# Projecting x by W1 and W2 during the first load of a four-layer graph kernel, and summing near rows straight into the residual

## The chip, the cores and the metric

The kernel runs on one core of one Trainium2 chip. The metric is the device time of one execution in microseconds (us); several executions are timed and their median is given. The profile is of one execution, whose span (first to last instruction) is a little shorter than its time.

## The reference, cut to what matters

There are N = 2708 nodes with D = 128 features each, and a dense f32 adjacency matrix `adj` of 2708 x 2708 (29 MB). Four graph layers follow one another, each wrapped as `x = layernorm(x + layer(x, adj))`. The change touches the first layer and the wrapping around it:

```python
def _lap_mul(A, x):
    d = 1.0 / jnp.sqrt(jnp.sum(A, axis=-1))
    return d[:, None] * (A @ (d[:, None] * x))

z = leaky_relu(_lap_mul(A, x) @ W1 + b1, negative_slope=0.1)
sq = jnp.sum(z * z, axis=-1)
d2 = jnp.maximum(sq[:, None] + sq[None, :] - 2.0 * (z @ z.T), 0.0)
S = jnp.exp(-jnp.sqrt(d2 + 1e-10) / 2.0)
S = jnp.where(ranks < 4, S, 0.0)      # the 4 nearest of each row
A2 = S + A
out = _lap_mul(A2, x) @ W2 + b2
x = layernorm(x + out)
```

So adj is multiplied twice: first for z, from which the 4 nearest rows of each row are found, and then, with those 4 entries added to each row, for the output. Layer 1 (an attention layer) ranks the rows by a score `c` that is computed from the x of layer 0; layers 2 and 3 each multiply adj once more.

## The kernel before, in words

Rows are cut into T = 22 tiles of 128 (the last, tile FULL = 21, has LAST = 20 rows). The columns of a product over all nodes are cut into C = 6 chunks: four of 512, one of 384 and one of 276 columns; `chunk_tiles` tells which row tiles a chunk covers (4, 4, 4, 4, 3 and 3). Products with adj have the transposed form: a tile of 128 rows of features is the stationary operand, 128 x 512 of adj (transposed in memory) streams past it, and a chunk's sum over all tiles stands in one PSUM bank `acc` (six of them; two further banks `mis` serve all else in the first stages). All matmuls are f32, and each is recorded in two parts. Six of the 22 row tiles of adj (`res`) stay in SBUF; the 16 others are streamed for each pass in panels of 4 tiles x 512 columns (`load_panel`, L157).

*The load and the first pass* (L425 to L504). For each chunk of columns, x (`load_x`) and the panels arrive by DMA. VectorE adds the panels up (`both`, L443 to L448), a matmul with `ones` (L460) turns that into row sums, the degrees; `inv_sqrt` makes `dinv`, and `scale_rows` writes `y = dinv * x` (L469). TensorE, in an order written out by hand (`manual_schedule`), forms what products it has data for (L392): a panel of chunk c can be used for the tiles whose `dinv` is known. When all is loaded, the panels that are still missing are fetched again (`rest`). At the end of a chunk, `finish` copies the sum to `hT`, `make_z` multiplies it by W1 (L344) and forms z and its norm on VectorE, `turn_z` transposes z back (L362), and `split_norms`/`turn_norms` cut the norm into three bf16 parts and turn them to a row (L371 to L384). Such later steps are queued in `Due`: `due.at(n, f)` runs f when the n-th product has been issued, `tick` counts products.

*The neighbour search* (L555 to L582). For each row tile, six bf16 matmuls with the norms (L564) and six f32 matmuls of z (L574) fill the six banks; ScalarE copies them to `key` (three buffers), and VectorE finds the eight largest and their places (L576, L577). `weigh` (L520), called for three groups of tiles, turns them to similarities `sim`, adds them to the degree, and writes `y2 = d2inv * x` to SBUF and to memory (`y2_rows`). The first groups are multiplied on GpSimd, the last on VectorE.

*Pass 2* (`by_panels`, L171, called at L776). The products of y2 with adj (L186), chunk by chunk. Beside them GpSimd fetches, for each row tile, the 4 nearest rows by 4 indirect DMAs (`sum_near`, L597; 16 buffers `got`), VectorE sums them weighted by `sim` into `near_sum` (L608, L610), and TensorE adds that to the chunk's sum by a matmul with the identity (`add_near`, L614). Then, per chunk: copy to `hT` (L733), `norm0` (times W2, add to x and b2, layer norm; L644), `turn` (transpose, L660), `find_c` (the score c, L668), and per tile `compare` (which scores are greater, L687), `rank_rows`, `rank_columns` and `times_w`. The numbers in `near_at` (L723) and in `end_pass2` say at which product each of these is issued. TensorE, VectorE and ScalarE work strictly in that order in this stage. Once all ranks are known, layer 1 goes on.

Of the kernel before, what the change touches and what calls it, by code (L numbers as in the profile page):

```python
# [50 lines left out]
def kernel(  # L51
# [73 lines left out]

    def load_x(ts):
        t0, t1 = ts[0], min(ts[-1] + 1, FULL)
        nc.sync.dma_start(xs[:, t0:t1, :], x[t0 * P : t1 * P, :].rearrange("(t p) d -> p t d", p=P))
        if t1 <= ts[-1]:
            nc.sync.dma_start(xs[:LAST, FULL, :], x[FULL * P :, :])  # L130
# [15 lines left out]
    hT = big.tile([P, N], F32, tag="hT", name="hT")  # L146
# [24 lines left out]
    def by_panels(weights, done, tick=None, ready=(), first=None, behind=None):  # L171
# [8 lines left out]
        def product(c, i, src, w):  # L180
# [4 lines left out]
            stop = tick is None and i == (FULL if c % GROUPS == 0 else FULL - 1)  # L185
# [51 lines left out]
    def add_bias(b):  # L237
        nc.vector.tensor_add(xs, xs, b[:, None, :].to_broadcast([P, T, D]))
# [26 lines left out]
    y = big.tile([P, T, D], F32, tag="y", name="y")  # L265
# [63 lines left out]
    with tc.tile_pool(name="knn", bufs=1) as knn:  # L329
        nsq = knn.tile([P, T], F32, tag="nsq", name="nsq")  # L330
        nsq3 = knn.tile([3, N], BF16, tag="nsq3", name="nsq3")
# [3 lines left out]
        nc.vector.memset(nsq, 0.0)  # L335
# [3 lines left out]
        zs = {}  # L339

        def make_z(ts):
            po = mis_tile()
            for k, t in enumerate(ts):
                nc.tensor.matmul(  # L344
                    po[: pw[t], k * D : (k + 1) * D], lhsT=hT[:, t * P : t * P + pw[t]], rhs=w1_sb, start=True, stop=True
                )
            for k, t in enumerate(ts):
                p = pw[t]
                z = zs[t] = knn.tile([P, D], F32, tag="z", name="z", bufs=8)
                nc.vector.scalar_tensor_tensor(  # L350
                    z[:p], po[:p, k * D : (k + 1) * D], dinv[:p, t : t + 1], b1_sb[:p], op0=ALU.mult, op1=ALU.add
                )
                nc.vector.scalar_tensor_tensor(z[:p], z[:p], 0.1, z[:p], op0=ALU.mult, op1=ALU.max)
                junk = small.tile([P, D], F32, tag="junk", name="junk")
                nc.vector.scalar_tensor_tensor(
                    junk[:p], z[:p], -1.0, z[:p], op0=ALU.mult, op1=ALU.mult, accum_out=nsq[:p, t : t + 1]
                )

        def turn_z(c, ts):
            pt = mis_tile()  # L360
            for k, t in enumerate(ts):
                nc.tensor.transpose(pt[:, k * P : k * P + pw[t]], zs[t][: pw[t]], ident[: pw[t], : pw[t]])  # L362
            nc.scalar.copy(zT[:, cols[c]], pt[:, : cw[c]])

        def split_norms(c, ts):

            t0, w = ts[0], len(ts)
            parts = small.tile([P, 4, 3], F32, tag="parts", name="parts")
            rest = small.tile([P, 4], F32, tag="rest", name="rest")
            part_b = small.tile([P, 4], BF16, tag="part_b", name="part_b")  # L370
            nc.vector.tensor_copy(rest[:, :w], nsq[:, t0 : t0 + w])  # L371
            for n in range(3):
                nc.vector.tensor_copy(part_b[:, :w], rest[:, :w])
                nc.vector.tensor_copy(parts[:, :w, n], part_b[:, :w])
                if n < 2:
                    nc.vector.tensor_sub(rest[:, :w], rest[:, :w], parts[:, :w, n])
            return parts

        def turn_norms(c, ts, parts):
            ps = mis_tile()  # L380
            for t in ts:
                o = t * P - starts[c]
                nc.tensor.transpose(ps[:3, o : o + pw[t]], parts[: pw[t], t - ts[0], :], ident[: pw[t], : pw[t]])
            nc.scalar.copy(nsq3[:, cols[c]], ps[:3, : cw[c]])  # L384
# [6 lines left out]
        def add(c, i, src, first=False, last=False):  # L391
            nc.tensor.matmul(accs[c][:, : cw[c]], lhsT=y[:, i, :], rhs=src[:, : cw[c]], start=first, stop=last)  # L392
# [12 lines left out]
        def add_few():  # L405
            for c in range(C):
                nc.tensor.matmul(
                    accs[c][:, : cw[c]], lhsT=y[few(c), FULL, :], rhs=res[few(c), FULL - S, cols[c]],
# [4 lines left out]
        def finish(c):  # L413
            ts = chunk_tiles[c]
            nc.scalar.copy(hT[:, cols[c]], accs[c][:, : cw[c]])
            due.at(due.n + 2, make_z, ts)
            due.at(due.n + 8, turn_z, c, ts)

            def norms():
                parts = split_norms(c, ts)  # L420
                due.at(due.n + 4, turn_norms, c, ts, parts)

            due.at(due.n + 7, norms)

        G = S // 4  # L425
        with (
            tc.tile_pool(name="load", bufs=4) as load,
            tc.tile_pool(name="degp", bufs=2) as degp,
            tc.manual_schedule(engines={nc.tensor.engine}),
        ):  # L430
            wait = None
            for c in range(C):
# [15 lines left out]
                nc.vector.tensor_add(both[:, 0, :w], both[:, 0, :w], both[:, 1, :w])  # L448

# [7 lines left out]
                ts = chunk_tiles[c]  # L457
# [11 lines left out]
                scale_rows(y, xs, dinv, ts)  # L469
                if c == C - 1:  # L470
                    spread(y[:, FULL, :])
                wait = (c, c, parts[c] if c < G else None, c == C - 1)
                if c == C - 2:
                    w1_sb = load_const(w1, D, "w1")
                    w2_sb = load_const(w2, D, "w2")
# [4 lines left out]
                    b1_sb = load_rows(b1, D, "b1")  # L480
# [24 lines left out]


# [10 lines left out]

        y2 = big.tile([P, T, D], F32, tag="y", name="y2")

        def weigh(ts):  # L520
# [14 lines left out]
            if t1 < T:  # L535
                nc.gpsimd.tensor_mul(  # L536
                    y2[:, t0:t1, :], xs[:, t0:t1, :], d2inv[:, t0:t1, None].to_broadcast([P, t1 - t0, D])
# [626 lines left out]
```

## Time and profile before

| what | us |
|---|---|
| time, median of 3 executions | 1121.94 (1120.0 to 1123.04) |
| span of the profiled execution | 1119.4 |
| TensorE busy (matmul) | 1044.2 |
| VectorE busy | 642.7 |
| ScalarE busy | 306.1 |
| GpSimd busy | 299.4 |

By stage (busy us of each engine in the stretch, and the share of the DMA engines):

| stretch (us from the span's start) | TensorE | VectorE | ScalarE | GpSimd | DMA |
|---|---|---|---|---|---|
| 0 to 56, load | 25.85 | 41.70 | 1.69 | 12.45 | 0.99 |
| 56 to 98.8, load | 42.60 | 33.32 | 0.62 | 0 | 0.97 |
| 98.8 to 149.8, rest of the first pass | 51.00 | 20.48 | 9.21 | 0 | 0.42 |
| 149.8 to 294, neighbour search | 142.69 | 136.36 | 79.04 | 5.63 | 0.03 |
| 294 to 301.8, into pass 2 | 6.39 | 3.84 | 1.42 | 3.80 | 0.65 |
| 301.8 to 414, pass 2 | 109.18 | 64.47 | 31.33 | 87.22 | 0.70 |
| 414 to 438, end of pass 2 | 13.58 | 19.70 | 12.36 | 3.60 | 0.11 |
| 438 to 1119, all later stages | 652.94 | 322.83 | 170.44 | 186.71 | |

The granted clock of TensorE is its share of full speed[...]. In a timeline each line is a run of like instructions: start, duration, engine, source line, operation, output and inputs, shapes, count, and in brackets the idle time before it with what ended it.

### The profile page before, as it was taken

Reading aid. Unit: us, or ns where it says so; the run is one execution under the profiler, and the core shown is the slowest. Engines: PE = TensorE matmul, PEld = TensorE weight load, DVE = VectorE, ACT = ScalarE, POOL = GpSimd, SP = SyncE. Lnnn points to the kernel's source line nnn. Section 1 sums busy time; section 2 is a strip of 40 time slices with the busy share of each in tenths; the row PEclk is TensorE's granted clock in tenths of the full one; section 3 lists DMA queues with packets and bytes.
Section 4 is the critical chain, followed back from the end, with each engine's and each line's share of the span. In section 5 each row is a group of like instructions: output and inputs, shape, how many; then the busy total and the mean of one; then the engine's idle time right before and its main releaser. Section 6 shows DMA issues by size and latency. Waiting matters only on the chain.

```text
span 1119.4 us, 10743 instructions
## 1 busy us (share of the span) xinstructions
PE 1044.2 (93%) x3495; PEld 494.5 (44%) x3495; DVE 642.7 (57%) x1381; ACT 306.1 (27%) x569; POOL 299.4 (27%) x296
## 2 busy tenths in 40 slices
PE   0899999999999975999799999998999999999997
PEld 0346544444345654333333333333444644465445
DVE  6885549999636679403099999997311212122132
ACT  0000145555202434000165656664110100011000
POOL 4000000000477772772355655660010100000000
PEclk9999999999999995999999999998999999998999
DMA  9996320000576660797545534454475766563754
GB/s 349 354 316 222 125 101 1 1 0 1 178 274 201 184 207 13 230 304 236 164 121 148 176 96 129 164 171 142 150 236 186 227 227 219 173 227 117 263 166 129
DMA packets 110245, 193.89 MB, mean 173 GB/s; under 512 B 14156, under 2 KB 47106, under 8 KB 109926
## 3 DMA queue, kind: packets, MB, share of 16 engines
q1 hardware_dynamic: 91046, 151.12, 40.7%
q0 software_dynamic: 19136, 42.01, 12.0%
q8 instruction: 29, 0.48, 0.2%
q14 instruction: 34, 0.28, 0.1%
HBM read 217.20 MB, written 4.30 MB: 198 GB/s over the span
## 4 chain that ended last, share of the span: by engine, by line
PE 51%; issue 4%; DMA 4%; DVE 2%; POOL 1%; ACT 1%; POOLq 0%; DVEq 0%; ACTq 0%
PE acc L186 32%; PE hacc L977 8%; PE num L1048 8%; DMA rows<-in_adjT,slot_i 2%; DMA part<-in_adjT 1%; PE mis L259 1%; POOL rows L1035 1%; DVE mask L692 1%; PE mis L1110 0%; PE mis L1063 0%; DMA got<-y_rows,where 0%; ACT junk L710 0%; ACT hT L220 0%; PE mis L1076 0%; DVE mask L697 0%
## 5 line engine op out<-in xcount | busy, mean ns | idle before, releaser
L186 PE MATMUL acc<-part,y 128*128 128x512 f32 (+2 forms) x384 | 156.0, 550 | 2.1 <-DMA part<-in_adjT 1.6
L1035 POOL DMA_INDIRECT rows<-in_adjT,slot_i x86 | 120.7, 1404 | 107.9 <-PE num L1048 79.9
L1048 PE MATMUL num<-rows,lw 128*64 128x512 f32 (+2 forms) x516 | 117.0, 558 | 6.7 <-DMA rows<-carry 3.7
L977 PE MATMUL hacc<-err,xws 128*128 128x512 f32 (+3 forms) x264 | 113.6, 567 | 2.2 <-DVE err L972 1.8
L574 PE MATMUL acc<-zT,z 128*128 128x512 f32 (+4 forms) x264 | 106.9, 552 | 0.0
L602 POOL DMA_INDIRECT got<-y_rows,where x88 | 93.0, 1057 | 29.6 <-issue 11.9
L186 PEld LDWEIGHTS acc<-part,y 128*128 128x128 f32 x384 | 70.4, 191 | 64.5 <-issue 53.9
L970 DVE TENSOR_TENSOR err<-inv,num 128x1024 f32<-128x1024 f32 (+1 forms) x88 | 74.5, 856 | 27.1 <-DMA rows<-in_adjT,slot_i 21.0
L966 ACT ACTIVATE inv<-num 128x1024 f32<-128x1024 f32 (+1 forms) x88 | 64.3, 734 | 88.4 <-PE num L1048 86.6
L575 ACT COPY key<-acc 128x512 f32<-128x512 f32 (+3 forms) x132 | 70.2, 534 | 58.1 <-issue 29.8
L392 PE MATMUL acc<-part,y 128*128 128x512 f32 (+2 forms) x192 | 82.4, 582 | 2.2 <-DVE y L233 2.2
L977 PEld LDWEIGHTS hacc<-err,xws 128*128 128x128 f32 (+1 forms) x264 | 47.1, 192 | 80.4 <-issue 41.8
L186 PE MATMUL acc<-part,lc 128*86 128x512 f32 (+2 forms) x192 | 76.2, 553 | 3.3 <-DVE lc L876 2.5
L186 PE MATMUL acc<-part,xs 128*128 128x512 f32 (+2 forms) x192 | 78.6, 552 | 0.1
L972 DVE SCALAR_TENSOR_TENSOR err<-gb,g_inv,err 128x1024 f32<-128x1024 f32 (+1 forms) x88 | 77.1, 918 | 0.0
L536 POOL TENSOR_TENSOR y<-xs,d2inv 128x2176 f32<-128x2176 f32 (+1 forms) x2 | 4.6, 2322 | 264.3 <-ACT d2inv L534 264.3
L186 PE MATMUL acc<-part,mixed 128*128 128x512 f32 (+2 forms) x192 | 75.0, 545 | 0.2 <-DMA part<-in_adjT 0.2
L971 DVE SCALAR_TENSOR_TENSOR err<-err,inv 128x1024 f32<-128x1024 f32 (+1 forms) x88 | 71.8, 857 | 0.0
L574 PEld LDWEIGHTS acc<-zT,z 128*128 128x128 f32 (+1 forms) x264 | 47.0, 186 | 53.8 <-issue 48.4
L220 ACT COPY hT<-acc 128x512 f32<-128x512 f32 (+2 forms) x18 | 9.6, 534 | 220.1 <-PE acc L186 203.2
L967 ACT ACTIVATE inv<-inv 128x1024 f32<-128x1024 f32 (+1 forms) x88 | 67.3, 768 | 2.6
L576 DVE MAX8 near<-key 128x8 f32<-128x2708 f32 (+1 forms) x22 | 65.3, 2970 | 3.4 <-ACT key L575 3.4
(239 smaller groups left out, 1215.5 us busy)
## 6 DMA issues: line engine op xcount, KB each, us to landing
part<-in_adjT SPq DMA_DIRECT2D x102, 1024.0 KB
part<-in_adjT SPq DMA_DIRECT2D x24, 768.0 KB
part<-in_adjT SPq DMA_DIRECT2D x24, 552.0 KB
res<-in_adjT SPq DMA_DIRECT2D x4, 1280.0 KB
got<-y_rows,where POOLq DMA_INDIRECT x88, 3.9
rows<-in_adjT,slot_i POOLq DMA_INDIRECT x86, 5.8
rows<-carry SPq DMA_DIRECT2D x86, 10.6 KB
xws<-by_rank POOLq DMA_DIRECT2D x1, 1365.0 KB, 10.1
```

Of the source, the lines that this page charges most:

```text
L186: nc.tensor.matmul(accs[c][: lhsT.shape[-1], :w], lhsT=lhsT, rhs=src, start=start, stop=stop)
L392: nc.tensor.matmul(accs[c][:, : cw[c]], lhsT=y[:, i, :], rhs=src[:, : cw[c]], start=first, stop=last)
L574: nc.tensor.matmul(pks[c][:p, : cw[c]], lhsT=z2[:, :p], rhs=zT[:, cs], start=False, stop=True)
L575: nc.scalar.copy(key[:p, cs], pks[c][:p, : cw[c]])
L602: nc.gpsimd.indirect_dma_start(out=got[:p, :], out_offset=None, in_=y2_rows[:, :], in_offset=bass.IndirectOffsetOnAxis(ap=where[:p, t, k : ...
L967: nc.scalar.activation(inv[:p], inv[:p], AF.Exp, scale=-1.0)
L970: nc.vector.tensor_mul(err[:p], inv[:p], num[:p, :w])
L971: nc.vector.scalar_tensor_tensor(err[:p], err[:p], 2.0, inv[:p], op0=ALU.subtract, op1=ALU.mult)
L972: nc.vector.scalar_tensor_tensor(err[:p], gb[:p, col : col + w], g_inv[:p, q : q + 1], err[:p], op0=ALU.max, op1=ALU.mult)
L977: nc.tensor.matmul(haccs[:, o:e], lhsT=xws[:p, q, :D], rhs=err[:p, o:e], start=(q == 0), stop=(q == NQ - 1))
L1035: nc.gpsimd.indirect_dma_start(out=rows[:KC, n, :], out_offset=None, in_=adj_half[:, :], in_offset=bass.IndirectOffsetOnAxis(ap=slot_i[h][ ...
L1048: nc.tensor.matmul(num[n * BJ : n * BJ + bw[b], o:e], lhsT=lw[:, b, : bw[b]], rhs=rows[:, n, c0 + o : c0 + e], start=True, stop=True,)
```

## The change

It uses that `(A @ (d * x)) @ W = A @ (d * (x @ W))`. The rows of x are multiplied by W1 and W2 once, during the first load: `turn_x` transposes them, `project` multiplies by both weights in one matmul of 256 columns, and ScalarE copies the products to `y1` and `y2`. The first pass then runs on `y1`, so that its sums are already the transposed z before scale and bias; `spread_dinv` writes `dinv` as a row on all partitions into `zT`, and `make_z` forms z there in place, without a product, transposes or `hT`. The norms of z come from one matmul of its squares with a column of -1, and their three bf16 parts are made on three rows. What `weigh` needs of the norms by row comes from a matmul of one column for each tile of the search (`nsq`). Pass 2 runs on `y2`, so `norm0` only transposes. `sum_near` adds the near rows, weighted by `sim * d2inv`, straight into the residual xs; `near_sum` and `add_near` are gone. For the last tile of 20 rows the 4 x 20 near rows are fetched by one gather (`few_got`) and added by one matmul with the weights `pick`. The bias b2 is added on GpSimd after the first pass. In the load, VectorE and ScalarE now also work in the written order. In pass 2, the numbers of `near_at` are new, and all that follows the sums of the last two chunks comes after the last product, in the order of a list.

The diff, cut to its core:

```diff
+    w12 = const.tile([P, 2, D], F32, tag="w12", name="w12")
+    nc.sync.dma_start(w12[:, 0, :], w1)
+    nc.sync.dma_start(w12[:, 1, :], w2)
...
     def add_bias(b):
-        nc.vector.tensor_add(xs, xs, b[:, None, :].to_broadcast([P, T, D]))
+        nc.gpsimd.tensor_add(xs, xs, b[:, None, :].to_broadcast([P, T, D]))
...
-        def make_z(ts):
-        def turn_z(c, ts):
-        def split_norms(c, ts):
-        def turn_norms(c, ts, parts):
+        def turn_x(c):
+            pt = mis_tile()
+            for k, t in enumerate(chunk_tiles[c]):
+                nc.tensor.transpose(pt[:, k * P : k * P + pw[t]], xs[: pw[t], t, :], ident[: pw[t], : pw[t]])
+            nc.scalar.copy(zT[:, cols[c]], pt[:, : cw[c]])
+        def project(ts):
+            po = mis_tile()
+            for k, t in enumerate(ts):
+                nc.tensor.matmul(
+                    po[: pw[t], k * 2 * D : (k + 1) * 2 * D], lhsT=zT[:, t * P : t * P + pw[t]],
+                    rhs=w12.rearrange("p s d -> p (s d)"), start=True, stop=True,
+                )
...
+        def spread_dinv(c):
+            ps = mis_tile()
+            for k, t in enumerate(chunk_tiles[c]):
+                p = pw[t]
+                nc.tensor.transpose(
+                    ps[:, k * P : k * P + p], dinv[:p, t : t + 1].to_broadcast([p, P]), ident[:p, :p]
+                )
+            nc.scalar.copy(zT[:, cols[c]], ps[:, : cw[c]])
+        def make_z(c):
+            z = zT[:, cols[c]]
+            nc.vector.tensor_mul(z, accs[c][:, : cw[c]], z)
+            nc.scalar.activation(z, z, AF.Identity, bias=b1_col[:, :1])
+            nc.vector.scalar_tensor_tensor(z, z, 0.1, z, op0=ALU.mult, op1=ALU.max)
+            sq = knn.tile([P, CW], F32, tag="sq", name="sq", bufs=2)
+            nc.scalar.activation(sq[:, : cw[c]], z, AF.Square)
+            return sq
+        def norms(c, sq):
+            w = cw[c]
+            ps = mis_tile()
+            nc.tensor.matmul(ps[:3, :w], lhsT=minus, rhs=sq[:, :w], start=True, stop=True)
...
         def finish(c):
-            nc.scalar.copy(hT[:, cols[c]], accs[c][:, : cw[c]])
-            due.at(due.n + 2, make_z, ts)
-            due.at(due.n + 8, turn_z, c, ts)
...
+            due.at(due.n + 6, norms, c, make_z(c))
...
-            tc.manual_schedule(engines={nc.tensor.engine}),
+            tc.manual_schedule(engines={nc.tensor.engine, nc.scalar.engine, nc.vector.engine}),
...
+                turn_x(c)
+                for n in range(0, len(ts), 2):
+                    due.at(due.n + 2 + n, project, ts[n : n + 2])
+                if c == 0:
+                    due.flush()
...
-                scale_rows(y, xs, dinv, ts)
+                scale_rows(y1, y1, dinv, ts)
...
+                due.at(due.n + 7, spread_dinv, c)
...
+                nc.tensor.matmul(
+                    nsq[:, t : t + 1], lhsT=nsq3[:, t * P : (t + 1) * P], rhs=ones3[:, :1], start=True, stop=True
+                )
...
     def sum_near(t):
-        g = near_sum[:p, t, :]
+        g = xs[:p, t, :]
...
-    def add_near(c, acc):
...
     def norm0(ts):
...
-                po[: pw[t], k * D : (k + 1) * D], lhsT=hT[:, t * P : t * P + pw[t]], rhs=w2_sb, start=True, stop=True
+            if t < FULL:
+                nc.tensor.transpose(out, turned, ident)
+            else:
+                nc.tensor.matmul(out, lhsT=turned, rhs=ident, start=True, stop=False)
+                nc.tensor.matmul(out, lhsT=pick, rhs=few_got, start=False, stop=True)
...
-    near_at = [28, 32, 37, 41] + [42 + (24 * (t - 4)) // 5 for t in range(4, 15)] + [97, 102, 109, 116, 123, 128, 131]
+    near_at = [17, 22, 28, 33, 39, 45, 50, 56, 61, 67, 73, 78, 84, 89, 97, 105, 113, 122, 131]
+    tail = T * C + 1
...
     def end_pass2(c, acc):
-        n = max(due.n + 1, near_at[chunk_tiles[c][-1]] + 3)
...
-        def finish():
-            add_near(c, acc)
-            nc.scalar.copy(hT[:, cols[c]], acc[:, : cw[c]])
-        at(n, finish)
+        at(due.n + 1, nc.scalar.copy, hT[:, cols[c]], acc[:, : cw[c]])
         if c < C - 2:
+            n = max(due.n + 1, near_at[ts[-1]] + 1)
             at(n + 2, norm0, ts)
             at(n + 9, turn, c)
             at(n + 11, find_c, c)
...
+            steps = [
+                (norm0, chunk_tiles[C - 2]), (turn, C - 2), (find_c, C - 2), (sum_near, ts[0]), (compare, a),
+                (rank_rows, a), (compare, b), (sum_near, ts[1]),
+                (gather, few_got, few_idx), (rank_rows, b), (norm0, ts),
+                *[(times_w, C - 3, t) for t in chunk_tiles[C - 3]],
+                (compare, d), (rank_columns, a), (rank_columns, b), (turn, c), (find_c, c), (rank_columns, d),
+                *[(times_w, C - 2, t) for t in chunk_tiles[C - 2]],
+            ]
+            for t in ts:
+                steps += [(compare, t), (times_w, c, t), (rank_rows, t)]
+            steps += [(rank_columns, t) for t in ts]
+            for n, step in enumerate(steps):
+                at(tail + n, *step)
```

## The prediction, written before the changed kernel ran

> **What bounds the kernel now.** I read the slices of the page first, then the timelines of TensorE, VectorE, ScalarE and GpSimd for the first 440 us (all that the diff touches), and last busy time by window. The slices:
>
> ```profile
> PE   0899999999999975999799999998999999999997
> DVE  6885549999636679403099999997311212122132
> DMA  9996320000576660797545534454475766563754
> ```
>
> A slice is 28 us. DMA is full for the first three (the load), DVE for the seventh to tenth (the neighbour search), PE nearly so from the third on. Which engine ends last is seen only in the timelines. The load and the first pass, TensorE (start, duration, line, count, in brackets the idle time before it):
>
> ```profile
> 40.05 12.24 PE L392 MATMUL acc<-part,y 128*128 128x512 f32 x24
> 55.30 1.02 PE L460 MATMUL mis<-ones,both 128*128 128x1 f32 x8 [3.00 <-DVE both L448]
> 56.19 15.68 PE L392 MATMUL acc<-part,y 128*128 128x512 f32 x32
> 72.06 1.02 PE L460 MATMUL mis<-ones,both 128*128 128x1 f32 x8 [0.20 <-DVE both L448]
> 72.95 14.00 PE L392 MATMUL acc<-part,y 128*128 128x384 f32 x40
> 86.78 0.73 PE L460 MATMUL mis<-ones,both 128*128 128x1 f32 x6
> 145.41 4.46 PE L392 MATMUL acc<-res,y 128*128 128x512 f32 x10
> ```
>
> Before 56 us TensorE waits for the row sums (3.00 us here), from 56 us on for nothing but 0.20 us: although DMA is full until 84 us, work added to TensorE after 56 us is paid. The search, one line of ScalarE, one of VectorE, one of TensorE:
>
> ```profile
> 243.01 1.50 ACT L575 COPY key<-acc 128x512 f32<-128x512 f32 x3 [0.27 <-PE acc L574]
> ```
> ```profile
> 244.54 2.98 DVE L576 MAX8 near<-key 128x8 f32<-128x2708 f32 x1
> ```
> ```profile
> 244.02 1.31 PE L564 MATMUL acc<-nsq,ones 3*128 3x512 bf16 x6
> ```
>
> The last key copy of a tile ends at 244.51 and its MAX8 starts at 244.54, though VectorE looks 99% busy. TensorE's period is 5.985 us (273.94 - 160.22, over 19 tiles), so TensorE sets the pace; only at the end, after the small operations of `weigh`, is VectorE behind (keys ready at 286.3, MAX8 at 287.29). Pass 2:
>
> ```profile
> 301.78 3.70 PE L186 MATMUL acc<-part,y 128*128 128x512 f32 x8 [1.41 <-DMA part<-in_adjT]
> 335.75 1.22 PE L664 MATMUL mis<-ident,xs 128*128 128x128 f32 x4 [1.47 <-DVE xs L251]
> 404.17 0.49 PE L619 MATMUL acc<-ident,near_sum 128*128 128x128 f32 x2 [1.44 <-DVE near_sum L610]
> 418.12 0.49 PE L619 MATMUL acc<-ident,near_sum 128*128 128x128 f32 x2 [3.85 <-DVE near_sum L610]
> ```
> ```profile
> 298.99 1.12 POOL L602 DMA_INDIRECT got<-y_rows,where  x1 [3.08 <-DMA y_rows<-y]
> 417.44 1.07 POOL L602 DMA_INDIRECT got<-y_rows,where  x1 [0.30 <-issue]
> ```
> ```profile
> 324.58 0.35 DVE L610 SCALAR_TENSOR_TENSOR near_sum<-got,sim,near_sum 128x128 f32<-128x128 f32 x1 [1.16 <-DMA got<-y_rows,where]
> ```
>
> Two streams run side by side: TensorE's products to 413.9, and 88 gathers on GpSimd, 1.30 us apart, to 418.5. The gathers end last. Then VectorE works nearly without a gap from 420.4 (mask of tile 16) to 437.4, and the ranks follow. After 438 us nothing is changed.
>
> **What the skill says.** "TensorE: Matmul & The Clock Gate", Part 1: after about one idle window of 3.4 us the array runs at half clock, until it has been busy as long. The trace agrees: the granted clock is 0.72 in 56:62, after the 3.00 us wait, and 0.57 in 337:341, after the 1.47 us wait, which costs about 1.75 us (337:340 holds 4 products' records in 3.37 us instead of 1.88). "GPSIMD Engine Reference", 3.1, puts an elementwise add at about twice VectorE's time. Here a 128x2176 product took 3.82 us on GpSimd, so the bias add over 128x2816 should take 4.9 us (against 3.09 on VectorE); GpSimd is idle from 13 to 277 us, which hides it.
>
> **The change part by part.** Net prices on TensorE from starts of neighbouring groups: four 128-column f32 matmuls 0.89 us, four transposes 0.44, one 512-column matmul 0.86, so a tile's 256-column projection 0.43.
>
> *Load, chunks 0 to 2.* Each gains `turn_x` 0.44, `project` 1.72, `spread_dinv` 0.44 on TensorE: 2.6 us. Chunk 0 lies in 23 us of idle time, the others largely in the waits of 1.8 and 3.0 us. VectorE is now in program order, so a chunk's sums can't start before the former chunk's degree, square root and scale; W1 and W2 go ahead of the first x (128 KB). With these, I put the row sums of chunk 2 at 55.7 instead of 55.15, chunk 3 starts 0.4 to 0.8 later: take +0.6. A wait less may also keep the clock up in one of two chunks (2 us): take -0.8, ends -2 and 0.
>
> *Load, chunks 3 to 5, on the path.* Ten transposes 1.1, ten projections 4.3, spreads of chunks 2 to 4 (11 tiles) 1.2: +6.6. ScalarE's copies (about 0.4 to 0.6 us each) lie beside two products of 0.86 us each, so no wait there.
>
> *98.8 to 149.8, TensorE without a gap.* Removed for five chunks (18 tiles): L344 4.2, L362 2.1, L383 2.0 = 8.3. Added: the norms matmul with 3 weight columns (priced by its 2192 moving columns in five chunks, at 0.86 per 512) 3.7, last spread 0.3. Net -4.3. The end of the first pass: +0.6 - 0.8 + 6.6 - 4.3 - 0.2 (the wait at 72.06) = +1.9 us.
>
> *Into the search.* Before, the first MAX8 came 11.1 us after the pass (149.8 to 160.94), through matmul, VectorE, transposes and ScalarE. Now z is made in place: I add product 0.7, ScalarE 0.6, leaky 0.6, square 0.6, norms matmul 0.9, two copies and two VectorE steps of 0.6 beside four products, and come to 10.5: -0.6.
>
> *Search.* One matmul of a single column per tile (`nsq`). The trace has none here; nearest are the L715 matmuls: 0.03 us for themselves, and the next pair of records grew from 1.02 to 1.10. So 0.03 to 0.15, I take 0.10: 21 x 0.10 = 2.1 on TensorE, of which 0.9 is VectorE's lag at the end (287.29 less 286.3, and a step of 0.1): +1.2. The small operations of `few_idx` and `pick` stand in VectorE's queue before the last y2 scale: +0.25.
>
> Sum up to the start of the gathers: 1.9 - 0.6 + 1.2 + 0.25 = +2.8 us. Panels and gathers of pass 2 both wait for y2's last rows and move alike.
>
> *Pass 2, TensorE from 301.78 to 413.88.* Removed: near sums of 19 tiles as matmuls 4.5; transposes in place of W2 products for chunks 0 to 3, 1.8; into the tail go norm0, turn and find_c of chunk 4, 1.6; and the waits 1.47 and 1.44. Together -10.8. Added: a new wait. `norm0` and `turn` of chunk 0 are now due at ticks 36 and 43 instead of 46 and 53, so TensorE reaches `turn` at 324.2 in the old time frame (tick 40 is at 321.2, 0.86 each, norm0's transposes 0.45). But tile 3's last row lands only at 324.58, because a gather took 5.9 us from its issue (318.65). Then near sum 0.35, four adds 1.1, statistics 1.7, square root 0.7, the first scaled tile 0.35: 328.9 to 329.8. TensorE, in order, waits some 5.2 us with all products behind it; the half clock afterwards was there before. Pass end: 413.9 - 10.8 + 5.2 + 0.5 (small gaps) = 408.8. The gathers of tile 18 (77 with the small one) are in by about 403: no longer the end.
>
> *Tail, on VectorE.* norm0 of chunk 4 3.6, turn and find_c with two ScalarE copies 2.8 at a cold clock, own 0.65, near sum 1.4, two compares 3.1, near sum 1.4, norm0 of chunk 5 3.6, its last compare 2.95, own 0.5, three compares 6.65 = 26.7, from 409.1: 435.8, where before it was 437.4. Pass 2 gains 1.6.
>
> Total: +2.8 - 1.6 = +1.2 us, so 1121.94 + 1.2 = 1123.1 us. I say 1123.
>
> **Rivals.** *No wait at the first turn* (gathers land in 3.9 us, the median, or TensorE arrives later). For: that median. Against: the heavy panel traffic at 308:336. Then 3 to 5 us come off; with a clock that stays up in the load 1121.9 + 1.2 - 4 - 1 = 1118. Faster. *TensorE binds the load harder*: both chunks cold (+0.8), ScalarE or buffer waits in program order (1 to 2), nsq at 0.15 (+1): 1121.9 + 1.2 + 4 = 1127. For: in-order queues on three engines; against: gaps of 0.86 us products cover the copies. Slower. *VectorE is relieved, and the tail shrinks*: the gathers were the last to end, so one could expect 4 to 8 us from their being off the end. Against: the VectorE tail takes over norm0 of chunk 4. It would give 1116.
>
> **How the numbers follow.** Small change 0.38 (the forecast); faster, by the first and third rivals 0.19 and 0.12, 0.31; slower, by the second, 0.31. The ends of the bounded costs against the values taken are: first pass -2 to +3, nsq -1.5 to +1, first wait -5 to +1.5, tail +/-2, hardly all to one side: 1114 to 1131 holds the time 8 times in 10.
>
> **What would show it.** Right: products end about 2 us later than 149.8; MAX8 spaced by 6.05 to 6.1 us; an idle time of about 5 us before the transposes of the first turn, released by VectorE; last gather before the end of VectorE's tail; the rank stage starting within 2 us of 438. Wrong: TensorE idle in chunks 3 to 5, a first pass that ends before 149 or after 154, no wait at the first turn, or a change after 438 us.

## The result, and the profile after

| | kernel before | changed kernel |
|---|---|---|
| time, median of 4 executions each, us | 1121.85 (1120.0 to 1123.04) | 1136.35 (1129.94 to 1136.74) |
| ratio, 95% interval | 1 | 1.0117 (1.0079 to 1.0156) |
| span of the profiled execution, us | 1119.4 | 1134.8 |
| mean granted TensorE clock | 0.971 | 0.961 |

The changed kernel is 1.2% slower, where 0.1% was forecast. Measured again in another session, the ratio was 1.0148 (1.0117 to 1.0178). In two of the four later sessions the kernel before itself took 1158.6 and 1160.0 us (in the one trace of it there, with an operation added, the gathers of pass 2 were issued over 141 us instead of 118), so a ratio is always to the kernel before in the same session.

The slices of the page, 28.4 us each:

```profile
PE   2898999999989995699989999999999999999997
DVE  5886327999935677800359999999221211223122
DMA  9995340000167662388735533453656667563754
```

The search, VectorE's row of nines, now lies in slices eight to eleven instead of seven to ten: the loss comes before it. Where, the slices don't tell; the timeline of TensorE in the load does (L475 are the row sums of a chunk, L411 products of the first pass, L363 the projections):

```profile
59.29 0.95 PE L475 MATMUL mis<-ones,both 128*128 128x1 f32 x8
76.47 0.95 PE L475 MATMUL mis<-ones,both 128*128 128x1 f32 x8
93.13 0.72 PE L475 MATMUL mis<-ones,both 128*128 128x1 f32 x6
97.15 0.61 PE L363 MATMUL mis<-w,zT 128*20 128x256 f32 x2
100.99 4.21 PE L411 MATMUL acc<-res,y 128*128 128x384 f32 x6 [3.23 <-DVE y L236]
105.63 6.42 PE L411 MATMUL acc<-part,y 128*128 128x276 f32 x24
113.28 0.64 PE L475 MATMUL mis<-ones,both 128*128 128x1 f32 x6
```

From chunk 2 to chunk 4 TensorE has no gap, as forecast. Between chunk 4 and chunk 5 it waits 3.23 us for `y1`, and three products (six records) then take 4.21 us, where the same three took 2.10 to 2.20 in the kernel before and in every variant below: half clock (0.51 in 100:106). VectorE and GpSimd, just before, and last the same scale on VectorE in the kernel before:

```profile
94.54 6.40 DVE L236 TENSOR_TENSOR y<-y,dinv 128x384 f32<-128x384 f32 x1
114.66 0.56 DVE L236 TENSOR_TENSOR y<-y,dinv 128x384 f32<-128x384 f32 x1
```
```profile
94.39 6.13 POOL L241 TENSOR_TENSOR xs<-xs,b 128x2816 f32<-128x2816 f32 x1 [81.59 <-PE mis L356]
```
```profile
88.19 0.56 DVE L233 TENSOR_TENSOR y<-xs,dinv 128x384 f32<-128x384 f32 x1
```

In the program text the bias add stands after the first pass, but nothing held it there: it started 68 us before the end of the pass, as soon as the transposes of chunk 5 (L356) had read x. The scale of chunk 4 takes 6.40 us, that of chunk 5, the same operation, 0.56. It starts 0.15 us after GpSimd's bias add and ends 0.4 us after it. The same pair comes a second time at the end of the search, when `sim` is scaled (L564) beside y2 (L549):

```profile
293.39 2.98 DVE L598 MAX8 near<-key 128x8 f32<-128x2708 f32 x1
296.29 3.14 DVE L564 TENSOR_TENSOR sim<-sim,d2inv 128x68 f32<-128x68 f32 x1
```
```profile
295.52 3.82 POOL L549 TENSOR_TENSOR y<-y,d2inv 128x2176 f32<-128x2176 f32 x1 [195.00 <-ACT d2inv L547]
```

MAX8, which starts before GpSimd's product and overlaps it, is not disturbed; the scale of 68 values per row, which follows it, ends with that product (299.43 and 299.34). And TensorE at the turn from the first pass to the search:

```profile
169.54 0.45 PE L595 MATMUL mis<-ones,nsq 3*128 3x1 bf16 x12
171.56 0.37 PE L583 MATMUL acc<-nsq,ones 3*128 3x512 bf16 x1 [1.58 <-DVE nsq L403]
173.87 2.43 PE L583 MATMUL acc<-nsq,ones 3*128 3x512 bf16 x6
176.23 7.70 PE L593 MATMUL acc<-zT,z 128*128 128x512 f32 x12
183.87 1.31 PE L583 MATMUL acc<-nsq,ones 3*128 3x512 bf16 x6
```

TensorE waits 1.58 us. Soon after, six norm products take 2.43 us instead of 1.31 and the six key products (twelve records) 7.70 instead of 4.81, with a granted clock of 0.62 in 176:184: the second tile of the search is nearly 4 us late.

The stages from mark to mark, two traces of each kernel ("repaired" is the changed kernel with the three repairs below; its second trace is of the experiment that adds products to pass 2):

| from the mark above to | before | changed | repaired |
|---|---|---|---|
| first panel added up by VectorE | 6.61, 6.78 | 9.10, 8.72 | 7.91, 7.63 |
| row sums of chunk 2 | 48.69, 48.32 | 50.19, 49.87 | 48.88, 48.68 |
| row sums of chunk 5 | 42.92, 43.85 | 53.99, 54.08 | 47.82, 47.83 |
| end of the first pass | 51.58, 51.57 | 49.20, 49.20 | 49.20, 49.20 |
| second MAX8 of the search | 17.13, 17.13 | 21.91, 21.94 | 17.39, 17.39 |
| last MAX8 | 120.36, 120.36 | 123.94, 123.95 | 121.01, 121.01 |
| first gather | 11.70, 11.72 | 12.22, 12.21 | 11.74, 11.74 |
| last rank product | 138.36, 138.35 | 137.45, 137.34 | 136.80, 137.59 |
| end of the span | 682.1, 680.5 | 676.8, 677.9 | 677.5, 683.2 |

The first gather comes 20 to 22 us later than before, not 2.8. The last line, stages that the change doesn't touch, differs by 6 us between the two traces of the repaired kernel, and the changed kernel had 681.5 in a third trace: it scatters too much to be set down to the change.

### The profile page after: what moved, and what is told of

Same layout as the page of the kernel before. It is cut to its first block, busy times and chain, and to the rows that moved or that the text cites. A ratio compares the mean times of both kernels' runs of the same rounds, so it can differ in the third digit from the quotient of the medians.

```text
span 1134.8 us, 10650 instructions
## 1 busy us (share of the span) xinstructions
PE 1057.6 (93%) x3466; PEld 495.7 (44%) x3466; DVE 643.9 (57%) x1274; ACT 325.9 (29%) x612; POOL 300.5 (26%) x297
## 4 chain that ended last, share of the span: by engine, by line
PE 45%; issue 2%; DMA 1%; DVE 1%; ACT 1%; POOL 0%; DVEq 0%; POOLq 0%
PE acc L189 24%; PE hacc L988 9%; PE num L1059 9%; PE mis L262 1%; PE mis L1121 0%; DMA rows<-carry 0%; PE mis L1074 0%; DMA rows<-in_adjT,slot_i 0%; DMA part<-in_adjT 0%; ACT hT L223 0%; PE mis L1087 0%; PE mis L1117 0%; DVE err L982 0%; ACT mT L1064 0%; DVE err L983 0%
## 5 line engine op out<-in xcount | busy, mean ns | idle before, releaser
L593 PE MATMUL acc<-zT,z 128*128 128x512 f32 (+4 forms) x264 | 111.2, 568 | 0.0
L189 PEld LDWEIGHTS acc<-part,y 128*128 128x128 f32 x384 | 71.0, 193 | 67.1 <-issue 52.8
L619 POOL DMA_INDIRECT got<-y_rows,where x84 | 89.5, 1066 | 28.9 <-issue 10.7
L411 PE MATMUL acc<-part,y 128*128 128x512 f32 (+2 forms) x192 | 81.2, 567 | 0.5 <-DVE y L236 0.5
L988 PEld LDWEIGHTS hacc<-err,xws 128*128 128x128 f32 (+1 forms) x264 | 46.5, 189 | 79.6 <-issue 43.7
L599 DVE FIND_INDEX8 where<-near,key 128x8 uint32<-128x2708 f32 (+1 forms) x22 | 65.4, 2972 | 0.0
```

The costliest lines, as they stand in the source:

```text
L189: nc.tensor.matmul(accs[c][: lhsT.shape[-1], :w], lhsT=lhsT, rhs=src, start=start, stop=stop)
L411: nc.tensor.matmul(accs[c][:, : cw[c]], lhsT=y1[:, i, :], rhs=src[:, : cw[c]], start=first, stop=last)
L593: nc.tensor.matmul(pks[c][:p, : cw[c]], lhsT=z2[:, :p], rhs=zT[:, cs], start=False, stop=True)
L619: nc.gpsimd.indirect_dma_start(out=got, out_offset=None, in_=y2_rows[:, :], in_offset=bass.IndirectOffsetOnAxis(ap=idx, axis=0), bounds_ch ...
L988: nc.tensor.matmul(haccs[:, o:e], lhsT=xws[:p, q, :D], rhs=err[:p, o:e], start=(q == 0), stop=(q == NQ - 1))
```

## The experiments

**Is it GpSimd's add that holds up VectorE?** Three kernels, measured together: the add on VectorE in idle time, the add on GpSimd in the fifth tile of the search, and an add put into the kernel before.

```diff
 def add_bias(b):
-    nc.gpsimd.tensor_add(xs, xs, b[:, None, :].to_broadcast([P, T, D]))
+    nc.vector.tensor_add(xs, xs, b[:, None, :].to_broadcast([P, T, D]))
...
                     rest(c, g, g == C - 1)
+                if c == 0:
+                    add_bias(b2_sb)
                 finish(c)
...
-        add_bias(b2_sb)
```

> The changed kernel with the bias add back on VectorE, in its idle time after chunk 1's norms (3.09 us there). Theory A (the GpSimd add, two inputs from SBUF, keeps VectorE's 128x384 scale of chunk 4 from running: 6.40 us instead of 0.56; TensorE waits 3.23 us for y1 and then runs six products and more at half clock): the scale takes 0.56 us again, the wait of 3.23 us before the products of chunk 5 goes, the first pass ends at 156 to 157.5 instead of 162.48, and the whole is 5 to 6 us faster than the changed kernel, about 1130.5. Rival B (the wait is one of the queues in program order and of TensorE's added work; the add only lies beside it): the wait of about 3 us stays, first pass end within 1 us of 162.5, time about 1136.

```diff
-        add_bias(b2_sb)
...
-                    nc.scalar.copy(key[:p, cs], pks[c][:p, : cw[c]])
+                    copied = nc.scalar.copy(key[:p, cs], pks[c][:p, : cw[c]]).ins
...
+                if n == 4:
+                    b2_late = knn.tile([P, D], F32, tag="b2_late", name="b2_late")
+                    with tc.issue_after(copied):
+                        nc.scalar.copy(b2_late, b2_sb)
+                    add_bias(b2_late)
```

> The changed kernel with the bias add still on GpSimd, but in the fifth tile of the search, where VectorE does only MAX8 and FIND_INDEX8, which read one tensor from SBUF. Theory A: it is the pair of operations with two inputs each that can't run together, so MAX8 and FIND_INDEX8 keep 2.97 us beside the add, and the kernel is as fast as the one with the add on VectorE, 1130 to 1131. Rival B: as the changed kernel, 1136. A third case (GpSimd holds up any VectorE operation): MAX8 or FIND_INDEX8 grow to 6 us or more and the search ends about 3 us later.

```diff
+            nc.gpsimd.tensor_add(
+                hT[:, : FULL * D].rearrange("p (t d) -> p t d", d=D), xs[:, :FULL, :],
+                b2_sb[:, None, :].to_broadcast([P, FULL, D]),
+            )
             assert (C, G) == (6, 4)
```

> The kernel before, with an additional GpSimd add of 128x2688 (x plus b2 into the still unused hT) that becomes ready when chunk 5's rows and b2 have landed, near 86 us; nothing reads its result. Theory A: VectorE's additions or the scale of chunk 4 stand still for up to the add's 5 to 6 us, chunk 5's row sums and the first pass end 2 to 6 us later, 1124 to 1128 in all. Rival B: GpSimd was idle there, so nothing moves: within 1 us of 1121.9.

In both kernels that move the add, chunk 4's scale takes 0.56 us, TensorE doesn't wait, and chunk 5's row sums follow chunk 2's after 47.8 us. The scale in the first of them:

```profile
91.41 0.56 DVE L236 TENSOR_TENSOR y<-y,dinv 128x384 f32<-128x384 f32 x1
```

It took 0.56 us in all twelve traces of variants without the add at that place, and 6.39 to 6.40 in all three of the changed kernel. With the add in the search, GpSimd and VectorE (timelines of the second kernel):

```profile
191.83 6.16 POOL L241 TENSOR_TENSOR xs<-xs,b_late 128x2816 f32<-128x2816 f32 x1 [176.98 <-ACT b_late L601]
```
```profile
191.58 2.98 DVE L596 MAX8 near<-key 128x8 f32<-128x2708 f32 x1
194.60 0.09 DVE L597 MATCH_VALUE_LOAD where<-near,key 128x8 f32 x1
194.68 2.97 DVE L597 FIND_INDEX8 where<-near,key 128x8 uint32<-128x2708 f32 x1
```

MAX8 starts just before the add; the two others start inside its 6.16 us, and none is longer than usual. And in the kernel before, with the added operation (GpSimd, VectorE, TensorE):

```profile
88.94 5.86 POOL L490 TENSOR_TENSOR hT<-xs,b 128x2688 f32<-128x2688 f32 x1 [76.41 <-DMA xs<-in_x]
```
```profile
90.53 4.68 DVE L233 TENSOR_TENSOR y<-xs,dinv 128x384 f32<-128x384 f32 x1
```
```profile
95.26 2.20 PE L392 MATMUL acc<-res,y 128*128 128x384 f32 x6 [2.89 <-DVE y L233]
```

Again the scale ends with the add (95.21 and 94.80), and TensorE waits 2.89 us; from chunk 4's row sums to chunk 5's it is 15.2 us instead of 11.4 and 12.8. So theory A holds and B falls, and so does the third case: what was held up in these traces are VectorE's TENSOR_TENSOR operations, with two inputs from SBUF, and not its operations with one. "SBUF — State Buffer", section "Who interferes with whom", of the Trainium skill says this: such an instruction and a GpSimd instruction that reads SBUF share an interface, and the second to issue stands still until the first has finished. The traces agree: the scale started second (0.15 and 1.59 us after the add) and ended 0.4 us after it. The whole times of these three could not tell how much each is worth: ratios of 1.0130 (1.0097 to 1.0163), 1.0132 (1.0097 to 1.0168) and 1.0022 (0.9984 to 1.0059), with no changed kernel beside them.

**The scaling of sim**, behind the issue of y_rows on GpSimd instead of on VectorE (`scaled` are its operands).

```diff
+            if t1 < T:
+                with tc.issue_after(ins.ins):
+                    nc.gpsimd.tensor_mul(*scaled)
+            else:
+                nc.vector.tensor_mul(*scaled)
```

> The bias add on VectorE in the idle time as in the first kernel of this group, and the scaling of sim of the first 20 tiles behind y2's on GpSimd instead of beside it on VectorE. Theory A: the scaling took 3.14 us at 296.29 because GpSimd's 128x2176 product ran until 299.34; moved, the last MAX8 and with it the gathers start 2.5 to 3 us earlier, and the whole is 2 to 3 us faster than with the bias add alone, about 1128. Rival B (scaling is slow by itself, a broadcast of 17 values over 68): GpSimd takes the time itself, and the search's end moves by no more than 1 us.

Measured ratio 1.0108 (1.0049 to 1.0168). From the second MAX8 to the last it is 121.01 us, in the changed kernel 123.94: 2.93 less. GpSimd did the scaling in 0.33 us, so it isn't slow by itself, and rival B falls. Beside the changed kernel:

> The changed kernel itself, beside the three below on the same chip, so that they can be compared with it and not only with the kernel before. Every theory: VectorE's scale of chunk 4 near 94 us takes 6 us again, the scaling of sim near 296 us takes 3 us, and the time is 0.8 to 1.6% above the kernel before.

> Bias add on VectorE in its idle time and sim's scaling behind y2's on GpSimd, beside the changed kernel on the same chip. Theory A (the two collisions cost 6 us before the first pass ends and 3 us at the end of the search): 8 to 10 us below the changed kernel, so within 0.6% of the kernel before. Rival C (the time of the first pass is given back in pass 2, whose gathers and panels are the bound): the gathers start 8 to 9 us earlier, yet the end comes at most 4 us earlier.

Ratios 1.0151 (1.0087 to 1.0216) and 1.0120 (1.0058 to 1.0183), in medians 7.5 us less, a little under the 8 to 10 expected; within 0.6% of the kernel before, as was also expected, it did not come. The intervals overlap, so the traces have to tell. In them the first gather came 12.6 us earlier and the last rank product 12.4 us (2.5 of it from the start, where the first panel came at 9.94 and 7.43): what is won before pass 2 isn't given back in it, so rival C falls.

**The turn.**

```diff
                         if c == 0:
+                            for _ in range(3):
+                                with tc.issue_after(made):
+                                    made = nc.tensor.matmul(
+                                        nsq[:, 32 : 32 + 448], lhsT=ident, rhs=zT[:, starts[2] : starts[2] + 448],
+                                        start=True, stop=True,
+                                    ).ins
                         norms(c)
...
-                    nc.tensor.matmul(pks[c][:p, : cw[c]], lhsT=z2[:, :p], rhs=zT[:, cs], start=False, stop=True)
+                    made = nc.tensor.matmul(
+                        pks[c][:p, : cw[c]], lhsT=z2[:, :p], rhs=zT[:, cs], start=False, stop=True
+                    ).ins
```

> As the kernel above, and three 448-column products without use on TensorE (2.2 us, their result is not read) in the wait before chunk 0's norms at the turn from the first pass to the search. Theory A (the wait of 1.58 us brings half clock over the next 10 us, 4 us lost): the six norm products after it take 1.31 us instead of 2.43 and the twelve key products 4.81 instead of 7.70, and the second MAX8 comes 6 us after the first instead of 9.8; 3 to 4 us less than the kernel above. Rival B (those products wait for keys or buffers, not for the clock): the second MAX8 stays 8.5 us or more behind the first.

TensorE at the turn, where L597 is the filling:

```profile
160.54 2.42 PE L597 MATMUL mis<-zT,ident 128*128 128x448 f32 x6
162.89 0.38 PE L586 MATMUL acc<-nsq,ones 3*128 3x512 bf16 x1
163.21 1.12 PE L603 MATMUL acc<-zT,z 128*128 128x512 f32 x2
164.26 0.17 PE L607 MATMUL mis<-ones,nsq 3*128 3x1 bf16 x1
164.30 1.30 PE L586 MATMUL acc<-nsq,ones 3*128 3x512 bf16 x6
165.53 4.81 PE L603 MATMUL acc<-zT,z 128*128 128x512 f32 x12
```

The norm products take 1.30 us and the keys 4.81: work that nobody needs makes the work behind it faster, and the second MAX8 comes 5.98 us after the first. So it does in all five traces with the filling (5.98 to 5.99), against 8.93 to 9.87 in the ten without. The wait's cost was the clock (1.00 in 160:171 here); rival B falls. The ratio is 1.0052 (1.0032 to 1.0072), in medians 4.9 us less than the kernel above, where 3 to 4 were expected.

**Program order on VectorE and ScalarE.** Beside the line shown, the bias add is on GpSimd in the search and sim's scaling is moved.

```diff
-            tc.manual_schedule(engines={nc.tensor.engine, nc.scalar.engine, nc.vector.engine}),
+            tc.manual_schedule(engines={nc.tensor.engine}),
```

> As the second kernel, with the bias add on GpSimd in the search, and with VectorE and ScalarE no longer kept in program order in the load (TensorE still is), so that the first sum of a chunk goes ahead of the former chunk's scale. Theory D (program order costs 1.2 to 1.4 us of VectorE for each of chunks 1 and 2, while TensorE waits for the sums): from the row sums of chunk 0 to those of chunk 2 32.2 us instead of 33.7, and the first pass ends 1 to 2 us earlier than with the second kernel. Rival (DMA sets that spacing): 33.5 us as before.

From chunk 0's row sums to chunk 2's it is 32.8 us, against 32.3 with order kept in the same session; the first pass ends 147.5 us after the first panel instead of 145.6; ratio 1.0103 (1.0058 to 1.0149). Nothing is gained: theory D falls.

**What the removed work brings in pass 2, and what the added work on TensorE costs in the load.** Both kernels have three repairs: the bias add on VectorE, sim's scaling moved, the turn filled. In the second of these, the first passes of chunks 3 to 5 run on x itself, which ScalarE copies in place of the products.

```diff
+    def again(t):
+        po = mis_tile()
+        nc.tensor.matmul(po[:, :D], lhsT=ident, rhs=y2[:, t, :], start=True, stop=True)
     for t in range(len(near_at)):
         at(near_at[t], sum_near, t)
+        at(near_at[t], again, t)
```

> The kernel with the three repairs, and in pass 2 one 128-column product without use on TensorE per tile of near rows, 19 of 0.22 us = 4.2 us, about what the near sums as products took before (4.5 us); nothing reads them. Theory E (the gathers end last in pass 2, so time taken off TensorE there is worth little): the last rank product comes no more than 1 us later. Rival F (TensorE's products set pass 2's end): 3 to 4.2 us later.

```diff
     def project(ts):
...
-            for k, t in enumerate(ts):
+            for k, t in enumerate(ts) if ts[0] < 12 else ():
...
```

> The kernel with the three repairs, without the products of x with W1 and W2 for the tiles of chunks 3 to 5 (ten products of 256 columns; ScalarE copies x itself in their place, so the first passes run on other numbers there). Theory G (in chunks 3 to 5 TensorE has no gap, and this work is paid in full): the row sums of chunk 5 follow those of chunk 2 after 43.5 us instead of 47.8, and the first pass ends 4.3 us earlier. Rival H (DMA or VectorE set the pace there and hide it): less than 2 us earlier.

Ratios 1.0043 (1.0022 to 1.0063) with the additional products, and 1.0031 (1.0006 to 1.0057) without the projections. Nineteen useless products in pass 2 left first gather to last rank product at 137.6 us, against 136.8 and 137.3 to 137.5 without them: theory E holds. The row sums without the projections:

```profile
56.14 1.02 PE L478 MATMUL mis<-ones,both 128*128 128x1 f32 x8 [0.27 <-DVE both L461]
72.13 1.02 PE L478 MATMUL mis<-ones,both 128*128 128x1 f32 x8 [0.30 <-DVE both L461]
87.57 0.72 PE L478 MATMUL mis<-ones,both 128*128 128x1 f32 x6
99.88 0.64 PE L478 MATMUL mis<-ones,both 128*128 128x1 f32 x6
```

43.7 us from chunk 2 to chunk 5 instead of 47.8, near the 42.9 and 43.9 of the kernel before: theory G, ten projections cost 4.1 us.

**Two small ones.** `spread_dinv` of chunk 5 was made due 16 products later instead of 7, and `few_idx` and `pick` were issued behind the last scale of y2. The first comes too late for chunk 5's z, which is then multiplied by other numbers.

> The kernel with the three repairs (bias add on VectorE, sim's scaling moved, the turn filled), and two small ones: chunk 5's spread of dinv no longer stands inside the products of the 20-row tile, and few_idx and pick come behind the last scale of y2 on VectorE. Theory A: the 20-row products of two groups of 8 and 4 take 1.98 us in one group instead of 2.9, and from the last FIND_INDEX8 to the last y2 scale 2.1 us instead of 3.1: together 1.5 us less than with the three repairs. Rival: both lie beside other waits, no change over 0.5 us.

The six 20-row products (twelve records) took 1.91 us to the next group, where four and two with the spread between them had taken 2.75, the spread not counted; from the start of the last FIND_INDEX8 to y2's scale it was 5.05 us instead of 5.55. By the first gather 0.6 and 0.1 us were left of this, where 1.5 were expected. Pass 2 was 140.3 us, and the ratio 1.0048 (1.0022 to 1.0074), no better than 1.0043 in the same session. The rival can't be excluded, and why pass 2 was longer stays open; with another z, other near rows are fetched in it.

> The kernel before once more, for its trace on the chip of the three below. Every theory: between the landing of the first panel and the first pass's end 143 us, as in its first profile; what the gathers take in pass 2 on this chip is read from it.

Its trace gave 143.7 us for the first pass (143.2 in the first profile), and the second column of "before" in the table.

**The three repairs, one after another, in one session.**

> The changed kernel again, with its trace, beside its three repairs. If what followed the ranks (676.8 us in its first trace, 680.5 to 683.3 in five other traces) is a property of the kernel, this trace gives 675 to 679 us again; if it is scatter of the transfers there, 680 to 684.

> The bias add on VectorE's idle time alone. Theory A: the first pass ends 6 to 7 us earlier after the first panel's landing than in the changed kernel; 5 to 6.5 us less in all if nothing is given back, 3 or less if a part is.

> The same with sim's scaling moved. Theory A: 2.9 us less from the second MAX8 to the last than in the changed kernel, and 2.5 to 3 us less in all than with the bias add alone.

> The same with the filled turn. Theory A: 3.5 to 4 us less than with two repairs, and the ratio to the kernel before 1.003 to 1.005, as with the useless products in pass 2 added (1.0043); if those products did cost something, 1.000 to 1.002.

| kernel | us | ratio to the kernel before (1121.76 us), 95% |
|---|---|---|
| changed | 1137.88 | 1.0148 (1.0117 to 1.0178) |
| bias add on VectorE in idle time | 1133.19 | 1.0094 (1.0059 to 1.0129) |
| and sim's scaling moved | 1130.40 | 1.0063 (1.0041 to 1.0085) |
| and the turn filled | 1126.31 | 1.0042 (1.0024 to 1.0060) |

In medians the three repairs bring 4.7, 2.8 and 4.1 us, 11.6 of the 16.1 that the changed kernel is slower here; by the ratios it is 6.1, 3.5 and 2.4. Neighbouring intervals overlap, so the times show the sum, and the traces the parts. For the first repair, by medians between the two cases expected, the end of the pass misleads: chunk 5's row sums followed chunk 2's after 47.75 us instead of 54.08, but 1.7 us went again before the end of the pass, with TensorE never idle and the granted clock at 0.72 in 112:118; the turn then took 1.6 us less, and at the second MAX8 the gain was 6.3 us again. After the ranks the changed kernel took 677.9 us once more; but so did the last kernel (677.5), and the second and third took 681.3 and 685.2. In 560:800 TensorE's products with the transferred rows waited 0 us for a transfer in the trace of the last kernel and 8.5 in that of the third, but 5.4 in that of the changed kernel and only 1.2 in the trace that gave 683.2: these waits alone don't decide it, and what does stays open. No version tried is faster than the kernel before.

## Why the prediction was wrong

The first gather was forecast 2.8 us later than before. With the three repairs it is 303.95 against 298.99 and 299.73, so 4.2 to 5.0 later, some 1.2 of which is the start of the load. The rest of the ledger was about right; what it lacked came on top. Three of the prediction's own signs of being wrong showed: TensorE idle in chunks 3 to 5, a first pass that ends after 154 us (162.5), and no wait at the first turn.

- **The step that failed: "GpSimd is idle from 13 to 277 us, which hides it."** The add's length was forecast as 4.9 us and measured as 6.13, twice the 3.09 on VectorE, which is not the point. I asked whether GpSimd had other work, and not what it shares with VectorE. VectorE's scale stood still for 6 us, with TensorE behind it at a place where it had no other work, and half clock afterwards. This cost 5.0 to 6.3 us: 52.8 to 54.1 in three traces instead of 47.8 from chunk 2 to chunk 5.
- **The scaling of sim was not priced at all.** It stands in the diff as a VectorE product added to `weigh`, beside the GpSimd product whose 3.82 us I had used as a price. This cost 2.9 us.
- **"Into the search", -0.6 us.** The chain of z and its norms was 12.1 us from the end of the pass to the first MAX8 instead of 10.5, and I did not ask what its last wait does to TensorE's clock: second MAX8 after 21.9 us instead of 17.1, 4.5 of it gone when the turn is filled (2.8 to 4.5 counted from all traces without the filling). "TensorE: Matmul & The Clock Gate", Part 1, of the Trainium skill, names one idle window of some 3.4 us; here 1.58 us without any product and 0.45 us with tiny ones were enough. The prediction said that its trace agreed with this page, but its own waits of 3.00 and 1.47 us, with a clock of 0.72 and 0.57 behind them, are shorter than that window too. The length of a wait doesn't settle it either way: after the 2.89 us in the kernel before with the added operation the clock stayed at 1.00 (95:98).
- Load, chunks 3 to 5: +6.6 less 0.8 for the clock and 0.2 for a wait forecast, +4.0 to 4.9 measured without the collision. The projections themselves were forecast at 4.3 us and cost 4.1.
- From chunk 5's row sums to the end of the pass: -4.3 forecast, -2.4 measured. The norm products cost 0.95 us each instead of 0.86, and chunk 5's spread splits the 20-row products (0.84 us). (The norm products of five chunks have 2196 moving columns, not 2192, which changes nothing.)
- Chunks 0 to 2: +0.6 forecast. With W1 and W2 ahead, the first panel came at 7.4 to 9.9 us in the changed kernel and its variants, at 6.6, 6.8 and 8.9 in the kernel before and its variant; from there to chunk 2 it took 48.3 to 50.2 us in the former and 47.6 to 48.7 in the latter. No run separates what W1 and W2 do in this from scatter.
- Search: one product per tile at 0.10 us forecast; 121.01 against 120.36 is +0.65 in all, +1.2 forecast.
- Pass 2: -1.6 forecast, -0.9 to -1.0 measured, by other ways than said, so that the near agreement is luck.

For that last point, pass 2 in the changed kernel (TensorE):

```profile
323.86 6.17 PE L189 MATMUL acc<-part,y 128*128 128x512 f32 x8 [4.36 <-DMA part<-in_adjT]
349.24 0.91 PE L689 MATMUL mis<-ident,xs 128*128 128x128 f32 x4 [0.35 <-DVE xs L254]
427.69 0.49 PE L671 MATMUL mis<-ident,hT 128*128 128x128 f32 x3
```

and VectorE at the start of the tail:

```profile
428.90 0.35 DVE L630 SCALAR_TENSOR_TENSOR xs<-got,sim,xs 128x128 f32<-128x128 f32 x1 [1.28 <-DMA got<-y_rows,where]
430.49 0.35 DVE L630 SCALAR_TENSOR_TENSOR xs<-got,sim,xs 128x128 f32<-128x128 f32 x1 [1.24 <-DMA got<-y_rows,where]
430.76 0.86 DVE L677 SCALAR_TENSOR_TENSOR xs<-mis,d2inv,xs 128x128 f32<-128x128 f32 x3
```

The wait of 5.2 us at the first turn didn't come (0.35): TensorE arrived later, after 4.36 us for a panel and four products (eight records) in 6.17 us at a low clock (0.63 in 323:331). Counted from the first gather, the products ended after 107.3 us (109.8 forecast), but the near rows of tile 18, forecast for about 104, landed after 109.9: the gathers still set the start of the tail, which then took 27.2 us as forecast (26.7). That fits the 4.2 us of useless products, which changed next to nothing.

So the rival that gave 1127, "TensorE binds the load harder", had the right side and the wrong reasons. None of the cases had one engine stopping another that it doesn't wait for. And repaired, the change was still 0.4% slower (0.2 to 0.6): it moves 4 us of work into the load, where TensorE has no gap, and takes work from pass 2, where the gathers end last.

## What to carry to other kernels

Work moved to an idle engine is hidden only if it takes nothing that a busy engine uses: look at what VectorE runs in that stretch, and put GpSimd's two-input operations beside VectorE operations with one input. Price a move by both ends: what the work costs where it goes, and whether the place that it leaves ends last. Where a chain of small steps hands over between engines, ask what the wait does to TensorE's clock: here 2.4 us of useless products in a wait brought the second MAX8 behind it 3 to 4.5 us forward in the traces.

## What the runs showed of the hardware that was not expected

- A VectorE operation beside GpSimd can stop as a whole: 6.40 us for 0.56, 3.14 where a sum of that size (L538) took 0.21, and 4.68 for 0.56, against no delay for MAX8 and FIND_INDEX8.
- TensorE's granted clock can fall without any idle time: to 0.72 in 112:118 of the kernel with only the bias add moved, behind the 20-row products. Why is not known.
- GpSimd can be the slower one too. The changed kernel's issue of a gather on GpSimd, beside two masks on VectorE:

```profile
425.65 1.91 POOL L619 DMA_INDIRECT got<-y_rows,where  x1 [0.30 <-DVE eq L724]
427.87 1.00 POOL L619 DMA_INDIRECT got<-y_rows,where  x1 [0.30 <-DVE xs L630]
```
```profile
424.01 1.22 DVE L722 TENSOR_SCALAR mask<-hT,cc 128x1920 bf16<-128x1920 f32 x1
425.41 1.28 DVE L722 TENSOR_SCALAR mask<-hT,cc 128x2048 bf16<-128x2048 f32 x1
```

  An issue takes 1.00 us, beside a mask 1.91. The same section of "SBUF — State Buffer" offers a reason: some one-input operations of VectorE also take the interface by which GpSimd writes its descriptors. No run here separates this from other causes.
- Six 20-row products (twelve records) on three groups of rows take 1.91 us together, and 2.75 us when other products stand between the fourth and the fifth.
